# Fewer multiplications in a graph network: two basis products in 15 block products, the second root product and the output product in 7

## The chip, the cores and the metric

The kernel runs on one core of one Trainium2 chip. The metric is the device time of one execution in microseconds (us). Three runs of the kernel before took 716.10, 716.02 and 715.76 us; their median is 716.02 us. One further execution was taken with the profiler, and every duration quoted here is from that one.

## The reference

A graph with 384 nodes and 12,672 edges goes through an attention layer (1024 features, 16 heads) and then through a relational network of two layers with 768 features. Only the second part matters here. All numbers are fp32.

```python
x = relu(h_text @ w_in + b_in)                   # [384, 1024] @ [1024, 768]
for l in range(2):
    h_in = x
    W = einsum('rb,bio->rio', comp[l], basis[l])  # 6 relations from 4 bases
    # messages per relation and edge, each divided by the count of its (relation, target),
    # summed by target; then:
    x = agg + h_in @ root[l] + conv_bias[l]
    x = relu(x) + h_in
    x = batchnorm(x)                             # over the 384 nodes
h_final = x @ w_out + b_out                      # [384, 768] @ [768, 1024]
out = x_after_attention + layernorm(h_final)
```

The kernel does not build the six relation matrices. It multiplies x with each of the four bases (four products of 384 x 768 with 768 x 768 per layer, called H), and it mixes the six count-normalised adjacency matrices A into four matrices At, one per basis, by the coefficients comp. The aggregate is then the sum over bases and nodes of At and H.

## The kernel before, in words

**Engines.** The matrix engine (PE) takes a stationary operand of 128 x 128 and a moving operand of 128 x N, and adds into one of eight PSUM banks. A `matmul` in the code shows as two records of PE in the profile. The vector engine (DVE) and the scalar engine (ACT) read PSUM and write SBUF. The order on PE, DVE, ACT, POOL and SP is the order of the Python code (`manual_schedule`), so an instruction that waits holds back all that stand behind it on its engine. A helper `next_bank` gives out the bank that has been out of use the longest.

**Block products.** Most products are already made by a scheme of Winograd: a product of 2 x 2 blocks takes seven block products in place of eight, and four sums on each side before them. Blocks are halves of the features, or of the nodes.

**Input product (L848 to L903).** It makes XT, x transposed, in three passes p of two feature tiles. In a pass the scalar engine copies a first block product out of PSUM, DVE adds a second one (`add_up_quad`, L882), and the scalar engine applies relu (L883); all further copies of the pass stand behind that relu on the scalar engine. After pass 0, DVE makes the four sums for pass 2 (`output_sums`, L396).

**The four bases of a layer (loop over b, L971 to L1010).** The 384 nodes are three tiles of 128. Two of them form the 2 x 2 scheme; the third is multiplied plainly. `node_sums` (L920) makes the four sums of x once per layer; `weight_sums` (L927, L929) and `last_sums` (L935) make the four sums of each basis. A basis is 33 matmuls with N = 384: 18 at L985 and 15 at L979. A basis comes from memory in three parts of 768 KB (`wload`, L85), into a pool of five buffers; SP issues a load when the buffer's last reader is done. Between the block products of layer 0, `share` (L361 to L367) turns counts into means, and `mix` (L346, L348) makes At. The counts are scattered by POOL until 386.3 us; then POOL issues twelve loads of them into the tile A.

**Root product and aggregate.** `pr[o]` receives root times x in 36 matmuls with N = 384 (L1019), and then a part of the aggregate in the same banks; `begin` copies it out. The aggregate's sums of At (L1082 to L1086) and of H (`feature_sums`, L1097), its products (`times`, L1077), the additions into XN (`take`, L1107), relu (`rectify`, L1110), the residual and the statistics (`measure`, L1042 to L1049) and the batch norm (`normalise_layer`, L1054 to L1058) follow in three passes p of two feature tiles.

**Output product (L1169 to L1198).** For each node tile t: 12 matmuls with N = 512 (tile 2: 6 with 512 and 12 with 256), then on DVE the addition of b_out, the statistics (L1187, L1189), and the layer norm with the residual (L1194 to L1197), then the store. `x_sb` holds the residual; POOL adds the layer norm's beta to it (L1170).

Of the kernel before, what the change touches and what calls it, by code (L numbers as in the profile page):

```python
# [10 lines left out]
F32 = mybir.dt.float32  # L11
# [6 lines left out]
P = 128  # L18
N = 384
# [9 lines left out]
HC = DC // 2  # L29
HN = N // 2  # L30
# [14 lines left out]

BQ, BK, BV, BIQ, BIK, BIV, B_IN, CB, GAM, BET, NCOL = 0, 8, 16, 24, 32, 40, 48, 54, 66, 78, 90
# [5 lines left out]
def gnn_kernel(ctx: ExitStack, tc: tile.TileContext, out, x, edges, chunks, cols, rows, small,  # L52
               wq, wk, wv, wiq, wik, wiv, wo, w_in, basis, root, w_out):
# [299 lines left out]
    def add_up(r):  # L353
        sums[r] = late.tile([P, N], F32, tag="sum", name="sum", bufs=4)
        nc.gpsimd.tensor_tensor(sums[r], A[:, r, 0, :], A[:, r, 1, :], ALU.add)
        nc.gpsimd.tensor_tensor(sums[r], sums[r], A[:, r, 2, :], ALU.add)

    def share(r):
# [3 lines left out]
        rn = late.tile([P, N], F32, tag="rn", name="rn", bufs=2)  # L362
# [9 lines left out]
    with ExitStack() as inner:  # L372
# [263 lines left out]
        A = late.tile([P, R, NT, N], F32, tag="A", name="A")  # L636

# [93 lines left out]
        for g in range(STEPS + 1):  # L731
# [14 lines left out]
            if f + 2 == STEPS:  # L746
# [4 lines left out]
                w_first = [wload(basis[0, 0, part], (2, DC), "w_c") for part in range(3)]  # L751
                w_first += [wload(basis[0, 1, part], (2, DC), "w_c") for part in range(2)]
# [117 lines left out]
        node_sum(T, 4, h2T, T4)  # L870
        rest = lambda: None
        for p in range(3):
# [23 lines left out]
            if p == 0:  # L896
                output_sums(a[2], S[0])

# [7 lines left out]
    with tc.tile_pool(name="conv", bufs=1) as cp:  # L906
# [7 lines left out]

        def node_sums(X):
            S = cp.tile([P, 4, 3, P], F32, tag="S", name="S")
            for i, a, b, op in ((0, block(X, 1, 0), block(X, 1, 1), ALU.add), (1, S[:, 0], block(X, 0, 0), ALU.subtract),
                                (2, block(X, 0, 0), block(X, 1, 0), ALU.subtract),
                                (3, block(X, 0, 1), S[:, 1], ALU.subtract)):
                nc.vector.tensor_tensor(S[:, i], a, b, op)  # L920
            return S

        def weight_sums(w):
            T13 = keep.tile([P, 3, 2, HC], F32, tag="hT", name="T13")
            T2 = keep.tile([P, 3, HC], F32, tag="mask8", name="T2")
            for c in range(3):
# [5 lines left out]
        def last_sums(w, T2):  # L932
            T4 = cp.tile([P, 3, HC], F32, tag="T4", name="T4")
# [4 lines left out]
        w_first = [w_first[:3], w_first[3:]]  # L938

        def load_basis(l, b):  # L940
            w = w_first.pop(0) if w_first else []
            return w + [wload(basis[l, b, part], (2, DC), "w_c") for part in range(len(w), 3)]
# [15 lines left out]

        def go_between(*site):
            between.pop(site, lambda: None)()  # L960

        S = node_sums(XT)
        w = load_basis(0, 0)
        T = weight_sums(w)
        for l in range(L):
# [3 lines left out]
            for b in range(B):  # L969
# [23 lines left out]
                times(pc, S[:, 0], lambda c: T[0][:, c], True)  # L993
# [3 lines left out]
                times(pa, S[:, 1], lambda c: T[1][:, c])  # L997
                nc.scalar.copy(hs[0][1], pa)
                times(pc, S[:, 3], lambda c: w[c][:, 1, HC:])
                nc.vector.tensor_tensor(hs[0][1], hs[0][1], pc, ALU.add)  # L1000
                times(pa, S[:, 2], lambda c: T[2][:, c])
# [12 lines left out]
            w = [wload(root[l, part], (2, DC), "w_c") for part in range(3)]  # L1014
            XN = xtp.tile([P, KC, N], F32, tag="XT", name="XN")
            pr = [next_bank("ps_c", [i for i in range(8) if i not in kept])[:, :N] for _ in range(KC)]
            for k in range(KC):
# [6 lines left out]
            room2 = keep.tile([P, KD * N], F32, tag="hT", name="room2")  # L1024
            spaces = [room2[:, 2304:]]
            if l + 1 < L:
                spaces += [v.rearrange("p i k o -> p (i k o)")[:, i * 768:(i + 1) * 768] for v, n in
                           ((cp.tile([P, 4, 3, P], F32, tag="S", name="sums"), 2),
                            (wpool.tile([P, 2, 6, P], F32, tag="w", name="sums"), 2)) for i in range(n)]
# [240 lines left out]
```

## Time and profile before

| | |
|---|---|
| median of three runs | 716.02 us |
| the profiled execution | 717.47 us |
| its span, first to last instruction | 715.7 us |
| PE busy | 699.9 us (98%) |
| DVE busy | 512.6 us (72%) |
| ACT busy | 157.6 us (22%) |
| POOL busy | 308.1 us (43%) |
| mean granted PE clock | 0.995 |

The span is what the page's shares refer to. The profiled execution's own time is 1.8 us longer than its span, and the median of the plain runs lies 0.3 us above the span.

How to read it: a stage has a stretch of time, and in it each engine has a busy time. Busy time of PE close to the length of the stretch means that PE was the limit there. "Idle before, releaser" tells how long an engine stood still ahead of an instruction, and what let it go on. A line ending in L402 or L85 is that of a helper used by many stages, so the tile's name tells the stage: ps_x is the input product, ps_g the bases, ps_c root and aggregate, ps_f the output.

### The profile page before, as it was taken

What the parts mean: (1) busy time and instruction counts of PE and PEld (TensorE: products, weight loads), DVE (VectorE), ACT (ScalarE), POOL (GpSimd) and SP (SyncE); (2) the same over time, 40 slices, a digit from 0 to 9 for tenths busy, and PEclk for the clock granted to TensorE, in tenths of its full rate; (3) what the DMA queues carried; (4) which work ended last, traced back from release to release, by engine and by line L of the source; (5) the groups of instructions that cost most, each with busy time, mean ns of one, the idle gap of its engine ahead of it and who ended that gap; (6) DMA issues with size and microseconds to landing.
All of it is one profiled execution on the core that took longest, in us unless ns stands there. A gap on an engine that the chain in (4) does not pass through costs nothing.

```text
span 715.7 us, 9149 instructions
## 1 busy us (share of the span) xinstructions
PE 699.9 (98%) x3228; PEld 527.9 (74%) x3228; DVE 512.6 (72%) x1307; ACT 157.6 (22%) x360; POOL 308.1 (43%) x239
## 2 busy tenths in 40 slices
PE   8999999999999999999999999999999999999995
PEld 7759999999997444478985555558975555579943
DVE  5886697868886699787534279798878766507756
ACT  3211111111111577410221124202131111011100
POOL 1366777778687788687786542000000000120000
PEclk9999999999999999999999999999999999999999
DMA  8788787373562622733424994311104322700001
GB/s 303 267 279 264 228 250 212 80 243 67 203 209 43 177 2 1 221 44 45 89 0 103 250 288 153 133 44 45 45 0 133 102 69 94 308 1 1 1 30 59
DMA packets 69180, 91.04 MB, mean 127 GB/s; under 512 B 22940, under 2 KB 50688, under 8 KB 68750
## 3 DMA queue, kind: packets, MB, share of 16 engines
q1 hardware_dynamic: 46830, 78.45, 32.6%
q0 software_dynamic: 21296, 9.60, 10.8%
q10 hardware_dynamic: 1008, 2.41, 0.9%
q8 instruction: 25, 0.41, 0.2%
q14 instruction: 21, 0.17, 0.1%
HBM read 79.27 MB, written 11.16 MB: 126 GB/s over the span
## 4 chain that ended last, share of the span: by engine, by line
PE 87%; DVE 10%; ACT 2%; DMA 1%; issue 0%; DVEq 0%; ACTq 0%
PE ps_g L985 12%; PE ps_g L979 10%; PE ps_k L402 10%; PE ps_c L1077 10%; PE ps_v L402 8%; PE ps_q L420 6%; PE ps_q L402 5%; PE ps_f L1183 4%; DVE At L348 4%; PE ps_y L402 3%; PE ps_c L1019 3%; PE ps_x L402 3%; PE ps_o L707 2%; PE ps_s L662 2%; PE ps_pT L696 2%; PE ps_v L586 2%
## 5 line engine op out<-in xcount | busy, mean ns | idle before, releaser
L283 POOL DMA_INDIRECT atab<-count,at x99 | 166.3, 1679 | 44.2 <-issue 23.5
L278 POOL DMA_INDIRECT mtab<-m_val,at x99 | 103.4, 1045 | 57.6 <-issue 22.9
L1170 POOL TENSOR_TENSOR x_sb<-x_sb,room 128x1024 f32<-128x1024 f32 x3 | 7.0, 2348 | 188.9 <-DMA room<-in_rows 188.9
L348 DVE SCALAR_TENSOR_TENSOR At<-A,small_sb,At 128x1152 f32<-128x1152 f32 x40 | 53.6, 1414 | 0.0
L979 PE MATMUL ps_g<-T,S 128*128 128x384 f32 x144 | 49.1, 486 | 0.0
L985 PE MATMUL ps_g<-w_c,XN 128*128 128x384 f32 x144 | 47.7, 487 | 1.1 <-DVE XN L1107 1.1
L985 PE MATMUL ps_g<-w_c,XT 128*128 128x384 f32 x144 | 47.9, 486 | 0.0
L420 PE MATMUL ps_q<-hT,w_q 128*128 128x384 f32 (+1 forms) x160 | 43.4, 435 | 1.4 <-DVE hT L108 1.4
L985 PEld LDWEIGHTS ps_g<-w_c,XN 128*128 128x128 f32 x144 | 27.3, 190 | 20.2 <-DVE XN L1107 1.4
L979 PEld LDWEIGHTS ps_g<-T,S 128*128 128x128 f32 x144 | 27.3, 190 | 19.2 <-ACT H L991 0.4
L985 PEld LDWEIGHTS ps_g<-w_c,XT 128*128 128x128 f32 x144 | 27.3, 190 | 18.8
L420 PEld LDWEIGHTS ps_q<-hT,w_q 128*128 128x128 f32 x160 | 30.1, 200 | 14.1 <-ACT hT L101 1.7
L1077 PE MATMUL ps_c<-At,H 128*128 128x192 f32 x216 | 36.4, 326 | 0.0
L1077 PEld LDWEIGHTS ps_c<-At,H 128*128 128x128 f32 x216 | 35.4, 190 | 0.5
L402 PE MATMUL ps_k<-T,S 128*128 128x192 f32 x192 | 35.1, 326 | 0.0
L1107 DVE TENSOR_TENSOR XN<-XN,ps_c 128x192 f32<-128x192 f32 x38 | 12.5, 349 | 30.8 <-ACT XN L1063 19.7
L402 PEld LDWEIGHTS ps_k<-T,S 128*128 128x128 f32 x192 | 31.8, 190 | 0.0
L1183 PE MATMUL ps_f<-w_out,XN 128*128 128x512 f32 (+1 forms) x84 | 31.1, 531 | 0.0
L675 DVE CUSTOM_DVE_ANT_0 s<-ps_s,mask 128x384 f32<-128x384 f32 x48 | 24.5, 550 | 5.3 <-PE ps_s L662 5.3
L267 DVE SCALAR_TENSOR_TENSOR same<-cells,own,later 128x128 f32<-128x128 int32 x99 | 28.0, 350 | 0.4
L267 DVE SCALAR_TENSOR_TENSOR same<-keys,key,weigh 128x128 f32<-128x128 int32 x99 | 27.9, 349 | 0.0
L1183 PEld LDWEIGHTS ps_f<-w_out,XN 128*128 128x128 f32 x84 | 15.9, 190 | 14.9 <-issue 14.3
(298 smaller groups left out, 1411.6 us busy)
## 6 DMA issues: line engine op xcount, KB each, us to landing
w_c<-in_basis SPq DMA_DIRECT2D x96, 192.0 KB, 4.1
atab<-zero SPq DMA_DIRECT2D x36, 192.0 KB, 5.2
A<-atab POOLq DMA_DIRECT2D x12, 576.0 KB, 9.0
keys<-keys_d SPq DMA_DIRECT2D x25, 192.0 KB, 5.1
w_c<-in_root SPq DMA_DIRECT2D x6, 768.0 KB, 7.1
w_q<-in_wiq SPq DMA_DIRECT2D x16, 256.0 KB, 6.4
w_k<-in_wk SPq DMA_DIRECT2D x16, 256.0 KB, 5.8
w_k<-in_wik SPq DMA_DIRECT2D x16, 256.0 KB, 3.0
```

Source lines behind the costliest of these rows:

```text
L267: nc.vector.scalar_tensor_tensor(same, row[:, n, :], mine[:, c:c + 1], times, ALU.is_equal, ALU.mult, accum_out=count[:, i, c:c + 1])
L278: nc.gpsimd.indirect_dma_start(mtab[c // PER][:, :], bass.IndirectOffsetOnAxis(at[:, 0, c:c + 1], 0), m_val[:, c:c + 1], None)
L283: nc.gpsimd.indirect_dma_start(atab[0 if i < 11 else i % 2][:, :], bass.IndirectOffsetOnAxis(at[:, 1, c:c + 1], 0), count[:, 1, c:c + 1], ...
L348: nc.vector.scalar_tensor_tensor(At[:, b], A[:, r], w, At[:, b], ALU.mult, ALU.add)
L402: nc.tensor.matmul(ps, a[:, k, :], b[:, k, :], start=start and k == 0, stop=(k == 3), skip_group_check=not start)
L420: nc.tensor.matmul(ps[o][:, c], wt_[:, k, o * P:(o + 1) * P], src[:, k, c], start=(k == 0 and c.start == 0), stop=(k == KD - 1 and c.stop ...
L675: nc.vector.tensor_tensor_reduce(s[j], ps[:, :N], mask8[:, t, :], -scale, 3.0e38, ALU.add, ALU.min, tops[:, j:j + 1])
L979: nc.tensor.matmul(ps, x[:, c], y(c), start=start and c == 0, stop=(c == 2), skip_group_check=not start)
L985: nc.tensor.matmul(ps, block(XT, n, i)[:, c], w[c][:, i, o * HC:(o + 1) * HC], start=(first and c == 0), stop=(c == 2 and (i == 1 or ps is ...
L1019: nc.tensor.matmul(pr[o], w[k // 2][:, k % 2, o * P:(o + 1) * P], XT[:, k, :], start=(k == 0), stop=(k == KC - 1))
L1077: nc.tensor.matmul(ps, x[:, c], y[:, c], start=start and c == 0, stop=stop and c == 5, skip_group_check=True)
L1183: nc.tensor.matmul(p, XT[:, k, t * P:(t + 1) * P], w[k // 2][:, k % 2, c0:c1], start=(k == 0), stop=(k == KC - 1))
```

## The change

1. **Bases 0 and 1 of layer 0** are made by a scheme for blocks of 3 x 2 and 2 x 3: three node tiles, two halves of the input features, three thirds of the output features. A plain product has 18 block products; the tables PRODUCTS, X_SUMS and W_SUMS give one with 15. Each block product is three matmuls with N = 256, added to one of four running sums c, each in a bank of its own; after a block product, the running sum is copied into, added to or taken from one or two of the nine output blocks of H. 11 sums of x are made once, 10 sums of weights per basis. DVE makes two sums of each kind in pass 1 of the input product, and the rest between the block products, by a table of steps. (A row of PRODUCTS names the block of x, the block of weights, the running sum, and the blocks of H with their signs.) In the second basis, DVE also makes `node_sums` and the first nine sums of basis 2, whose loads move ahead as well.
2. **The root product of layer 1** is made by the 2 x 2 scheme in three passes: 63 matmuls with N = 192. DVE's sums of At for the aggregate move between its passes; the sums of x and the first sums of root move into basis 3, and the part of the aggregate that was added in the root's banks gets three banks of its own.
3. **The output product** is made by the 2 x 2 scheme for node tiles 0 and 1: 21 matmuls with N = 512 in place of 24. Tile 2 stays plain. Its sums of weights are made by DVE during the aggregate of layer 1, its sums of x ahead of the product.
4. Layer norm's beta is added to x_sb by DVE in the three passes of the input product (128 x 1024 each); the row is loaded into boB before. POOL's three additions at L1170 go.
5. Tiles that were allocated anew (T13, T2, S, T4, sums) become fixed places: room2, mroom, x_all, w_room, sum_room.

```diff
+X_SUMS = (
+    (6, 1, 2, -1, 4),
+    (7, -1, 5, -1, 6),
...
+W_SUMS = (
+    (6, 1, 2, 1, 5, -2),
+    (7, 1, 1, 1, 6, -1),
...
+PRODUCTS = (
+    (2, 1, 0, ((4, 1),)),
+    (6, 6, 1, ((7, 1), (8, -1))),
+    (7, 7, 0, ((7, 1),)),
+    (5, 8, 2, ((7, 1),)),
+    (9, 9, 1, ((6, -1),)),
+    (10, 10, 0, ((8, -1),)),
+    (3, 4, 3, ((4, 1),)),
+    (11, 5, 0, ((5, -1),)),
+    (12, 12, 3, ((3, -1),)),
...
+    (0, 15, 3, ((1, -1),)),
+    (16, 3, 0, ((6, -1),)),
+)
...
-                w_first = [wload(basis[0, 0, part], (2, DC), "w_c") for part in range(3)]
-                w_first += [wload(basis[0, 1, part], (2, DC), "w_c") for part in range(2)]
+                for b, t in ((0, 2), (0, 1), (0, 0), (1, 2), (1, 1)):
+                    load_third(b, t)
+                nc.sync.dma_start(boB, rows[R_LNB:R_LNB + 1, :].to_broadcast([P, D]))
...
             if p == 0:
                 output_sums(a[2], S[0])
+            elif p == 1:
+                for i, x in enumerate(X_SUMS):
+                    if x[0] in (6, 14):
+                        sum_features(i)
+                for i in range(2):
+                    sum_weights(0, i)
+                    free_from[0, i] = 99
+            nc.vector.tensor_tensor(x_sb[:, p, :], x_sb[:, p, :], boB, ALU.add)
...
+        def bases_by_15():
+            todo = [(g * NPROD + w[5], 1, g, i) for g in range(BY_15) for i, w in enumerate(W_SUMS) if g or i > 1]
...
+            todo += [(first[x[0]] - 3, 2, 0, i) for i, x in enumerate(X_SUMS) if x[0] not in (6, 14)]
+            todo = sorted(todo + [(NPROD + k, 3, 0, 0) for k in (4,)] + [(NPROD + k, 4, 0, c) for c, k in enumerate((7, 8, 13))])
+            for step in range(NPROD * BY_15):
...
+                while todo and todo[0][0] <= step:
...
+                x, w, c, targets = PRODUCTS[k]
...
+                for j in range(3):
+                    nc.tensor.matmul(ps, x[:, j], w[:, j], start=start and j == 0, stop=(j == 2),
+                                     skip_group_check=not start)
+                for to, sign in targets:
...
+                    if (g, to) in begun:
+                        nc.vector.tensor_tensor(dst, dst, ps, ALU.add if sign > 0 else ALU.subtract)
+                    elif sign > 0:
+                        nc.scalar.copy(dst, ps)
...
+                if (g, k) == (0, 7):
+                    load_third(1, 0)
+                elif (g, k) in ((0, 10), (0, 14), (1, 8)):
+                    basis_loads.append(wload(basis[0, len(basis_loads)], (2, DC), "w_c"))
...
+        def second_root(rest):
+            root_w.append(wload(root_thirds[2], (KC, HC2), "w_c"))
...
+            for p in range(3):
...
+                times(pa, root_block(p, 0, 0), x_quarter(0, 0), True)
+                nc.scalar.activation(quads[0][0], pa, AF.Identity, bias=bs[0])
+                rest()
+                times(pb, root_block(p, 0, 1), x_quarter(1, 0), True)
+                nc.vector.tensor_tensor(quads[0][0], quads[0][0], pb, ALU.add)
+                times(pc, s[:, 0], T[0], True)
+                nc.scalar.activation(quads[1][1], pc, AF.Identity, bias=bs[1])
+                if p < 2:
+                    root_S.append(root_sums(p + 1))
+                times(pa, s[:, 1], T[1])
+                nc.scalar.activation(quads[0][1], pa, AF.Identity, bias=bs[0])
+                times(pc, s[:, 3], x_quarter(1, 1))
+                nc.vector.tensor_tensor(quads[0][1], quads[0][1], pc, ALU.add)
+                if p:
+                    next(shares_)
+                times(pa, s[:, 2], T[2])
+                nc.vector.tensor_tensor(quads[1][1], quads[1][1], pa, ALU.add)
+                if p:
+                    next(shares_)
...
+                out_sums((0, 0), (1, 0), (0, 1), (1, 1))
...
+                if l + 1 == L:
+                    out_sums(*(((0, 2), (1, 2), (2, 2), (3, 2)) if last else ((2, p),)))
                 times(pc, S[p][3], q(1, 1))
...
+                if l + 1 == L:
+                    out_sums((3, p))
...
-        for t in range(NT):
-            nc.gpsimd.tensor_tensor(x_sb[:, t, :], x_sb[:, t, :], rowsB[:, 2, :], ALU.add)
...
+        third(*parts[0], *range(KC - 1))
+        pa, pb, pc, pd = [next_bank("ps_f") for _ in range(4)]
+        times(pa, block(XT, 0, 0), b_end(0, 0), True)
+        put_out(0, 0, pa, True, False)
+        times(pb, block(XT, 0, 1), b_end(1, 0), True)
+        put_out(0, 0, pb, False, True)
+        times(pc, OS[0], summed(0), True)
+        put_out(1, 512, pc, True, False)
+        times(pa, OS[1], summed(1))
+        put_out(0, 512, pa, True, False)
+        times(pc, OS[3], b_end(1, 1))
+        put_out(0, 512, pc, False, True)
+        times(pd, block(XT, 1, 1), summed(3), True)
+        put_out(1, 0, pd, True, False)
+        times(pa, OS[2], summed(2))
+        finish(0)
+        put_out(1, 0, pa, False, True)
+        put_out(1, 512, pa, False, True)
+        third(*parts[0], KC - 1)
+        for p, c0 in parts[1:]:
+            third(p, c0, *range(KC))
+        finish(1)
+        for p, c0 in parts:
+            put_out(2, c0, p, True, True)
+        finish(2)
```

`put_out` is one DVE addition out of PSUM, with two statistics of 256 columns where its last argument says so. `finish(t)` is the layer norm and the store of node tile t, the same instructions as L1194 to L1198.

## The prediction

> **What bounds the kernel now.** I read the page first: the span, the busy times and the chain by engine.
>
> ```profile
> span 715.7 us, 9149 instructions
> PE 699.9 (98%) x3228; PEld 527.9 (74%) x3228; DVE 512.6 (72%) x1307; ACT 157.6 (22%) x360; POOL 308.1 (43%) x239
> PE 87%; DVE 10%; ACT 2%; DMA 1%; issue 0%; DVEq 0%; ACTq 0%
> ```
>
> PE is busy 98% of the span, so work taken from PE is worth its time unless another engine then comes last. DVE at 72% is the candidate. Then the busy times by stage (columns: PE, PEld, DVE, ACT, POOL, with instructions, then PE clock, DMA share, GB/s): input product, bases 0, 1 and 2, aggregate of layer 1, output product, tail.
>
> ```profile
> 341.11:370.89 29.78, 29.14 (x177) 28.02 (x177) 12.21 (x25) 7.97 (x22) 23.43 (x16) 1.00 0.34 49
> 370.89:392.18 21.29, 21.29 (x67) 12.55 (x67) 10.73 (x18) 2.81 (x6) 14.88 (x10) 1.00 0.38 63
> 392.18:413.45 21.27, 21.27 (x67) 12.53 (x67) 7.43 (x13) 2.87 (x6) 12.13 (x12) 1.00 0.97 254
> 413.45:434.76 21.31, 21.31 (x68) 12.47 (x67) 16.87 (x16) 6.05 (x12) 10.45 (x11) 1.00 1.03 270
> 636.34:677.29 40.95, 40.95 (x253) 40.95 (x253) 24.36 (x69) 6.78 (x16) 0.00 (x0) 1.00 0.00 1
> 677.29:708.20 30.91, 30.91 (x84) 15.61 (x83) 18.13 (x44) 1.13 (x4) 0.00 (x0) 1.00 0.09 34
> 708.20:715.70 7.50, 0.02 (x1) 0.00 (x0) 4.08 (x9) 0.20 (x1) 0.00 (x0) 0.78 0.19 71
> ```
>
> In these stages PE never rests, and DVE has 10 to 14 us to spare in each. The DMA share near 1 in bases 1 and 2 is POOL's loading of A. The chain in order of time (start, length) gives PE's pace and one place where DVE already decides:
>
> ```profile
> 355.88 0.28 DVE XT L882
> 356.18 0.36 ACT XT L883
> 356.54 0.32 ACT XT L888
> 356.90 11.98 PE ps_x L402 x72
> ...
> 370.89 11.61 PE ps_g L985 x36
> 677.29 30.94 PE ps_f L1183 x84
> ```
>
> The timeline of DVE shows one wait for weights in base 2, and the last addition of the output product:
>
> ```profile
> 418.74 0.96 DVE L927 TENSOR_TENSOR T<-w_c 128x768 f32<-128x768 f32 x1 [3.70 <-DMA w_c<-in_basis]
> 708.26 0.42 DVE L1187 TENSOR_TENSOR hf<-ps_f,room 128x256 f32<-128x256 f32 x1 [1.70 <-PE ps_f L1183]
> ```
>
> [...] 11.61/36 is 322.5; for N = 192, 162.5 (68.90 us for 424 records in the chain: 162.5). [...] N = 256 is 216 ns (16 records of L840 took 3.45 us) and N = 512 is 429. [...] 768 columns take 952 ns and 384 take 558, a slope of 1.03 ns. [...] w_c loads landed after 2.2 to 14.2 us, the late ones beside A's.
>
> **What PE saves.** Bases 0 and 1: 66 records of 322.5 are 21.29 us each; 45 matmuls, 90 records of 216.5, are 19.49. Two bases: -3.6. Root: 72 x 322.5 = 23.22; 126 x 162.5 = 20.48: -2.7. Output: 30.94; the scheme has 42 records of N = 512 and tile 2 has 12, so 54 x 429 + 24 x 216.5 = 28.37: -2.6. In all -8.9 us.
>
> **What comes back.** For each touched stretch I laid out the instructions in the changed order: each starts when its engine is free and its inputs are there. Durations are the rows' own (DVE 768 columns .95, 384 .56, 512 .69, 1152 1.36, PSUM addition .35 at 192 columns and .42 at 256; ACT .41), DVE instructions overlap by .07 where independent, a handover takes .05, and a PSUM result follows the next start by .16. Laid out so, the old input product ends at 370.80 (370.72 measured), and the old stretch from the second root to the last DVE instruction has the output product start 66.1 us in (65.9) and the tail end 35.41 us later (677.12 to 712.54 is 35.42).
>
> *Input product, +1.2.* Beta's addition (1.22 us, the row of L540) stands on DVE between the sums and pass 1's first addition, which starts right behind the sums (the 355.88 above). Behind it wait relu, the copy at L888, and PE at 356.90. Nothing hides 1.22 less .07 overlap. In passes 1 and 2 the additions and four early sums (4.1 us) end before PE needs what follows. POOL's removed additions hid behind PE: 0. The row's DMA comes after 20 loads that SP ends at 343.1; landing 6.2 us later, it is there before 356; the cover is 6 us.
>
> *Bases 0 and 1, +2.0.* DVE's work per pair: 18 weight sums (17.1), 9 sums of x (5.0), node_sums (2.2), basis 2's sums (4.5), 20 additions (8.4): 37 us in 39. A product reads a running sum's bank only after the last copy from it. So PE waits where DVE is behind: at product 8 of base 0 for the addition of product 6 (.3), and at product 7 of base 1, because between products 3 and 5 DVE has node_sums and two weight sums, 4.1 us, ahead of product 5's addition, and PE offers 3.9 less what was late already: 1.05. Last, base 2's first matmul takes the bank that base 1 used first; its wait on DVE stands in the changed order. That bank's last addition follows the last product: .16 + .05 + .42 + .05 = .7, where before the next basis followed at once.
>
> *The late weights, +0.6.* Ahead of that addition DVE has the third part of basis 2's sums. Its load can go out only when product 7 of base 1 has freed a buffer, at about 403.3 on the old clock. Loads beside A's took 7.2 us here (411.5, when basis 1's buffer came free, to 418.7) and 8.6 (387.04 to 395.68). So the part lands at 410.5 to 411.9; DVE gets there at 410.6. Waiting 0 to 1.3, I take .6. Before, this wait held DVE alone; now it holds PE. Then DVE enters base 2 with the sums done, 4.5 us and the old 3.70 us wait ahead; shares and mix have more room, but the mix starts after base 3 in any case and is as long as before: 0.
>
> *Second root and aggregate, +1.5.* Basis 3 gets 5.2 us more DVE on 12.8 in 21.4: covered. In the root, the last addition of pass 1 stands behind a sum of At (1.36): .2, and .1 at the start. In the aggregate, DVE goes from 24.4 to about 33 us in 41, by 12 sums of w_out (.69 each). Where such a sum stands ahead of a `take`, PE waits for the bank: in pass 1 .2 and .4, in pass 2 .5. Three new takes and the early sums of At hide.
>
> *Output and tail, +3.7.* PE ends 28.4 us after the product's start, not 31.0, but DVE is the later one. Tile 1's last blocks and tile 2 come out together: pd ends at 19.75 us, and from 19.96 DVE has in this order: one addition (.62), finish(0) 3.33, two blocks with statistics 1.44 each, finish(1) 3.33, tile 2's three parts 1.44 + .81 + .88, and finish(2) 3.32: 16.6 in all, with no wait for PE. It ends at 36.55, where the old tail ended at 35.41. So the stretch is 1.1 longer, and PE's 2.6 is lost too.
>
> **Sum.** -8.9 + 1.2 + 2.0 + 0.6 + 1.5 + 3.7 = +0.1 on a span of 715.7. The median of the plain runs stands 0.3 above that span; +0.1 on 716.02 is 716.1 us. Changes below 0.2% (1.4 us) are about what this measurement cannot tell from none.
>
> **Rivals.**
>
> *PE's saving mostly arrives.* My waits in bases and aggregate hang on .2 to 1 us of DVE lateness; if DVE catches up there, 2.0 + .6 + 1.5 fall away, and 716.1 becomes 712.0. For it: before, DVE waited for PE 31.2 us at L1000. Against it: the layout met the old times within .2. If also the tail were no longer than PE's, 708.3; its DVE list is too plain for that.
>
> *The late part of basis 2.* This one ends slower. Loads beside A's took up to 14.2 us. Landing at 416 in place of 411.2 puts 4.8 us on PE's path at the start of base 2: 720.9. It decides from a landing at 412.6 on, which brings 717.5. For it: DMA share .97 to 1.03 there. Against it: the three loads ahead of it go out before 392, so less is queued.
>
> *DVE does not keep up in the bases.* 37 of 39 us leaves little; dependent sums cost .1 more each. Ten such would make 717.1.
>
> That the change removes nothing can be excluded: the order has the 45 matmuls per basis.
>
> **How the numbers follow.** The forecast, gains eaten: .50 (714.5 to 717.6 its own range); saving mostly arrives, 710 to 714.5: .24; late part or slow bases, 717.5 to 722: .22; full saving .02; worse .02. The range 712.3 to 719.6 leaves out about a fifth. Faster by over 0.2% (below 714.6): .27; slower (above 717.4): .25; between: .48.
>
> **What would show it.** In the chain: DVE XT ahead of PE in pass 1 about 1.2 us later; waits of PE ps_g on DVE H of about 1 us at product 7 of base 1 and .7 or more at base 2, with DVE T idle for w_c just before; base 2 starting between 413.0 and 414.3. The last PE matmul some 8 us ahead of DVE's last instruction, not 4.5; DVE without gaps there. The prediction is wrong if PE waits for neither, or if the last part lands after 412.6.

## The result, and the profile after

The changed kernel took 720.7 us (median of 13 runs, 716.4 to 724.25), the kernel before beside it 716.05 us (13 runs, 715.76 to 717.84). The ratio is 1.0056, with a 95% interval of 1.0039 to 1.0072: slower by over 0.2%, and outside the range given. Here and below, a ratio and its interval compare only those runs of each kernel that lie within 1.5% of its own fastest run. The profiled execution took 722.45 us.

The page of the changed kernel gives the span, the busy times and the chain by engine:

```profile
span 720.7 us, 9459 instructions
PE 693.3 (96%) x3324; PEld 541.5 (75%) x3324; DVE 557.5 (77%) x1385; ACT 160.2 (22%) x372; POOL 302.4 (42%) x236
PE 80%; DVE 14%; ACT 2%; issue 1%; DMA 1%; SPq 0%; DVEq 0%; ACTq 0%
```

PE is busy 6.6 us less (8.9 were forecast; slower matmuls, shown below, take back 2.6) and DVE 44.9 us more, and DVE's share of the chain went from 10% to 14%. Who held PE between 330 and 470 us stands in the waits (total, times, longest, in us):

```profile
PE ps_g L1244 <- DVE H L1100: 5.5, 1, 5.5
PE ps_x L452 <- ACT XT L980: 1.2, 1, 1.2
PE ps_g L1094 <- DVE H L1100: 0.7, 1, 0.7
```

The 1.2 us in the input product and the 0.7 us inside the bases were forecast. The 5.5 us stand before base 2's first matmul, where 1.3 were forecast (0.7, and 0.6 for the late weights). DVE's timeline there (start, length, line, output and inputs, idle time before it):

```profile
408.02 0.75 DVE L1100 TENSOR_TENSOR H<-H,ps_g 128x256 f32<-128x256 f32 x2 [0.54 <-PE ps_g L1094]
412.65 1.77 DVE L1033 TENSOR_TENSOR room<-w_c 128x768 f32<-128x768 f32 x1 [3.88 <-issue]
414.45 1.23 DVE L1035 TENSOR_TENSOR mroom<-w_c,room 128x384 f32<-128x384 f32 x1
415.61 0.41 DVE L1100 TENSOR_TENSOR H<-H,ps_g 128x256 f32<-128x256 f32 x1
```

L1033 and L1035 are the two sums of the third part of basis 2, L1100 below them is the addition that frees the bank. DVE first stands idle for 3.88 us, with no releaser that the profile could name, and then takes 3.0 us for sums that take 0.95 and 0.56 elsewhere. At the same time POOL's timeline has a sum of A (L405), which took 1.58 us in place of 0.99:

```profile
412.89 1.30 POOL L911 DMA_DIRECT2D A<-atab  x1
413.69 1.58 POOL L405 TENSOR_TENSOR sum_room<-A 128x384 f32<-128x384 f32 x1
415.34 1.20 POOL L406 TENSOR_TENSOR sum_room<-sum_room,A 128x384 f32<-128x384 f32 x1
```

What follows the pause is dear too. Busy times by stretch (PE, PEld, DVE, ACT, POOL, then PE clock, DMA share, GB/s):

```profile
400.00:408.00 8.00, 8.00 (x37) 7.07 (x38) 6.86 (x11) 1.51 (x4) 5.49 (x5) 1.00 1.03 196
408.00:416.00 8.00, 2.57 (x12) 1.91 (x11) 4.07 (x6) 0.38 (x1) 3.83 (x4) 0.90 1.06 371
416.00:424.00 8.00, 7.93 (x17) 4.49 (x18) 1.90 (x4) 0.56 (x1) 5.10 (x6) 0.67 1.14 265
```

Between 416 and 424 PE is busy and makes 17 records, at a mean granted clock of 0.67: up to 421.3 its records of 384 columns start 0.640 us apart, and 0.3225 after that.

By stages, from the first matmul of one to the first of the next (from the two traces):

| stage, us | before | after | change | forecast |
|---|---|---|---|---|
| input product | 29.78 | 30.91 | +1.13 | +1.2 |
| four bases of layer 0 | 87.99 | 93.84 | +5.85 | -1.0 |
| rest of layer 0 | 69.00 | 69.00 | 0 | 0 |
| bases of layer 1 | 83.31 | 83.31 | 0 | 0 |
| second root and aggregate | 66.11 | 64.58 | -1.53 | -1.2 |
| output product to the end | 38.57 | 39.64 | +1.07 | +1.1 |
| from the input product on | 374.75 | 381.27 | +6.52 | +0.1 |

The input product itself began 1.5 us earlier (339.40, not 340.94), which makes +5.0 of the span. The bases of layer 0 hold all of the miss.

### The profile page after: what moved, and what is told of

It reads as the page before. It is cut to its first block, busy times and chain, and to the rows that moved or that the text cites. A ratio compares the mean times of both kernels' runs of the same rounds, so it can differ in the third digit from the quotient of the medians.

```text
span 720.7 us, 9459 instructions
## 1 busy us (share of the span) xinstructions
PE 693.3 (96%) x3324; PEld 541.5 (75%) x3324; DVE 557.5 (77%) x1385; ACT 160.2 (22%) x372; POOL 302.4 (42%) x236
## 4 chain that ended last, share of the span: by engine, by line
PE 80%; DVE 14%; ACT 2%; issue 1%; DMA 1%; SPq 0%; DVEq 0%; ACTq 0%
PE ps_k L452 10%; PE ps_g L1244 10%; PE ps_v L452 8%; PE ps_g L1238 8%; PE ps_c L1347 7%; PE ps_q L470 6%; PE ps_q L452 5%; DVE At L398 4%; PE ps_g L1094 4%; PE ps_y L452 3%; PE ps_x L452 3%; PE ps_c L1182 3%; PE ps_o L758 2%; PE ps_f L1479 2%; PE ps_s L713 2%; PE ps_pT L747 2%
## 5 line engine op out<-in xcount | busy, mean ns | idle before, releaser
L470 PE MATMUL ps_q<-hT,w_q 128*128 128x384 f32 (+1 forms) x160 | 41.8, 422 | 1.4 <-DVE hT L158 1.4
L470 PEld LDWEIGHTS ps_q<-hT,w_q 128*128 128x128 f32 x160 | 28.5, 190 | 14.1 <-ACT hT L151 1.7
L1244 PE MATMUL ps_g<-w_c,XT 128*128 128x384 f32 x72 | 26.9, 527 | 5.5 <-DVE H L1100 5.5
L1244 PEld LDWEIGHTS ps_g<-w_c,XT 128*128 128x128 f32 x72 | 14.8, 208 | 16.5 <-DVE H L1100 5.9
L1238 PE MATMUL ps_g<-room,x_all 128*128 128x384 f32 x72 | 25.2, 486 | 0.0
L1281 PE MATMUL ps_c<-XT,w_c 128*128 128x384 f32 x72 | 23.5, 486 | 0.0
L758 PE MATMUL ps_o<-At,v 128*64 128x384 f32 x96 | 20.8, 512 | 1.3 <-ACT attT L761 1.3
L713 PE MATMUL ps_s<-k,q 64*128 64x384 f32 x96 | 21.5, 528 | 0.0
L416 DVE RECIPROCAL sum_room<-sum_room 128x384 f32<-128x384 f32 x6 | 15.3, 2549 | 7.5 <-ACT sum_room L415 7.5
L1033 DVE TENSOR_TENSOR room<-w_c 128x768 f32<-128x768 f32 x18 | 17.9, 996 | 3.9 <-issue 3.9
```

Source lines behind the costliest of these rows:

```text
L470: nc.tensor.matmul(ps[o][:, c], wt_[:, k, o * P:(o + 1) * P], src[:, k, c], start=(k == 0 and c.start == 0), stop=(k == KD - 1 and c.stop ...
L713: nc.tensor.matmul(score[g][j][:, :N], q2[ho, hc, t * P:(t + 1) * P], k2[ho, hc, :], start=True, stop=True)
L758: nc.tensor.matmul(pso[p][j * HD:(j + 1) * HD, :N], v2[:, m, h * HD:(h + 1) * HD], turned(g)[:, j, :], start=(m == 0), stop=(m == NT - 1))
L1238: nc.tensor.matmul(ps, x[:, c], y(c), start=start and c == 0, stop=(c == 2), skip_group_check=not start)
L1244: nc.tensor.matmul(ps, block(XT, n, i)[:, c], w[c][:, i, o * HC:(o + 1) * HC], start=(first and c == 0), stop=(c == 2 and (i == 1 or ps is ...
```

## The experiments

In most of the runs below the stages ahead of the input product were longer, and the kernel before took longer beside them too (medians of 728 to 750 us in place of 716, which is called its usual pace below); their times scattered by 10 us and more. So I compare the stages from the input product's first matmul, each from one profile: those that nothing touched were 69.0 and 83.3 us in every profile. The code cuts are shortened. "Base 0 to 2" is the stretch from base 0's first matmul to base 2's.

### Is it the load?

`e8_A_later`: the block that loads A goes behind the bases in the code, and POOL waits for base 1.

```
+ if (g, k) == (1, 13): nc.gpsimd.tensor_copy(scrap, H_[:, 1, targets[0][0] // 3, :1])
- (ahead of the input product) all nc.gpsimd.dma_start(A[...]) and add_up
+ (behind bases_by_15) the same
```

> The changed kernel with POOL's loads of A held back until product 13 of base 1 (POOL copies one column of H first, and the loads stand behind it), about 17 us later than before. Nothing but the third part's load is then under way from 401.5 to 408.5. Theory 'the late part': the load lands in 4 to 5 us, before DVE gets there at 408.8, DVE's idle time ahead of that sum is 0 to 0.3 us, and PE waits at most 2.5 us before base 2 (the part's two sums, 1.5 us, and the addition still stand there). Rival (DVE's 3.9 us are not the load, as the profile names no releaser for them): the idle time stays at 3 us or more. The whole time tells nothing here: the shares of A come 17 us later and PE will wait for them in base 2 or 3.

DVE's timeline:

```profile
429.53 0.95 DVE L1025 TENSOR_TENSOR room<-w_c 128x768 f32<-128x768 f32 x1
430.52 0.56 DVE L1027 TENSOR_TENSOR mroom<-w_c,room 128x384 f32<-128x384 f32 x1
```

No idle time, usual lengths, and PE waited 0.5 us. Base 0 to 2 took 40.8 us. The load's last piece landed at 427.09 in the trace, 4.7 us after its first was issued and 2.4 us before DVE came. (PE later waited 7.7 us for the shares of A, as had to be expected.) That takes away A's transfers and A's sums together; the next run parts them.

`e13_only_A_sums`: the loads of A stay, and only POOL's sums of them wait for base 1.

```
- for r in range(R): accumulate A[r]; load the next; if 0 < r < 5: add_up(r - 1)
+ for r in range(4): accumulate A[r]; load the next
+ if (g, k) == (1, 12): nc.gpsimd.tensor_copy(scrap, H_[:, 1, targets[0][0] // 3, :1])
+ (behind the bases) for r in range(4): add_up(r); if r > 1: accumulate A[r + 2]
```

> The changed kernel with POOL's sums of A held back until product 12 of base 1, and nothing else: the third part's sums stay ahead of the last addition. It parts the two causes. If the load's landing matters by itself, DVE stands idle ahead of that sum and PE's wait before base 2 is above 2.0 us; if the landing is in time, the two sums (1.5 us) start at about 0.6 us ahead of the last product's end and PE waits 1.4 to 1.6 us, the stretch from base 0 to base 2 taking 41.6 to 41.9. Theory 'both': up to the last product the stretch is 40.2 to 40.4, as clean as in the kernel with both repairs, and what is above comes from the wait for the load alone. Rival (POOL's sums don't matter without the other repair): 42 or more up to the last product.

```profile
414.31 0.96 DVE L1031 TENSOR_TENSOR room<-w_c 128x768 f32<-128x768 f32 x1 [3.66 <-issue]
415.30 0.56 DVE L1033 TENSOR_TENSOR mroom<-w_c,room 128x384 f32<-128x384 f32 x1
```

The sums have their usual length again, but DVE idles as long as before, and PE waits 3.8 us. Up to the last product the stretch is 40.3 us, as "both" said; bases 2 and 3 took 47.1 us, 1.6 above 45.5, at a clock of 0.79 behind the pause. Timed: 1.0061 (1.0031 to 1.0091). So the idle time is the load, even though the profile calls it "issue". The trace's landings agree: the part comes in four pieces, the last of which landed at 412.57 in the changed kernel and at 414.23 here, 0.08 us ahead of DVE's start each time.

`e9_as_changed`: the changed kernel once more.

> The changed kernel once more, as it is, for a second trace of bases 0 and 1. Theory 'the late part' with 'POOL and DVE slow each other' (a DVE sum of two tensors in SBUF is made late by a sum of A that POOL is making, and the reverse): PE waits 2 to 6 us before base 2, its length differs from the first trace's 5.5 us with what of A's transfers and sums falls beside it, and each DVE sum that takes more than 1.2 times its usual time overlaps a sum of POOL's (lines L405 and L406). Rival (DVE slows beside transfers): slow DVE sums stand where POOL makes no sum.

PE waited only 1.0 us before base 2, but 2.2 and 0.9 us inside base 1; base 0 to 2 took 43.9 us, where the first trace had 45.8. The late sums and POOL's:

```profile
443.64 2.36 DVE L1035 TENSOR_TENSOR mroom<-w_c,room 128x384 f32<-128x384 f32 x1
445.92 1.75 DVE L1033 TENSOR_TENSOR room<-w_c 128x768 f32<-128x768 f32 x1
```

```profile
444.04 1.54 POOL L405 TENSOR_TENSOR sum_room<-A 128x384 f32<-128x384 f32 x1
445.65 1.20 POOL L406 TENSOR_TENSOR sum_room<-sum_room,A 128x384 f32<-128x384 f32 x1
```

Every slow DVE sum of the stretch overlaps a sum of POOL's. So PE is held up by two causes, in shares that change from run to run.

### Is it the place in DVE's queue, and the bank?

`e1_sums_last` moves the third part's sums behind the last addition:

```
- [(NPROD + k, 4, 0, c) for c, k in enumerate((7, 8, 13))]
+ [(NPROD + k, 4, 0, c) for c, k in enumerate((7, 8))]
+ (behind the loop over products) third.append(weight_sums(basis_loads, 2))
```

> The changed kernel with one step moved: the third part of basis 2's sums (T13(2) and T2(2)) is made after the last addition of base 1, not before it. Theory 'the late part' (DVE stands at that sum until the part's load has landed, and the addition that frees base 2's first bank stands behind it): PE's wait before base 2 falls from 5.5 us to about 0.7, the clock granted after it is 1.00 again in place of 0.67, so some 4.8 + 2.8 us leave the profiled execution (722.45): 714 to 715.5, and the runs, which spread from 716.4 to 724.25, come within about 2 us of each other. Rival 'DVE is late as a whole' (its work for bases 0 and 1 has piled up, and the sum is only where it shows): the addition is still late, PE waits 3 us or more, 718 or more. Rival 'the time is lost elsewhere' (tail, aggregate): the wait goes and the median stays above 718.

`e2_other_bank` leaves DVE's order and turns the five banks of base 2 by one, so that `pa` gets a free one:

```
+ if (l, b) == (0, BY_15): five = five[1:] + five[:1]; taken[:] = taken[1:] + taken[:1]
```

> The changed kernel with another bank for base 2's first matmuls: pa gets one that base 0 had freed, and the bank that base 1's last product adds up in goes to pc, which starts some 11 us later. DVE's order stays. Theory 'the late part': PE no longer waits at base 2's start (0 to 0.1 us), while DVE still stands idle for 2 to 5 us ahead of the third part's sum; the time is 713.5 to 715.5, as with the sums moved or 0.7 less. Rival (PE needs what DVE makes there, or the weights themselves are late for PE): PE waits 3 us or more at another matmul of base 2, and the time stays above 718.

With the sums last, PE waited 0.52 us before base 2; with the other bank 0 us, although DVE still idled 1.1 us ahead of the sum. In both, bases 2 and 3 took 45.5 and 45.4 us (48.08 in the changed kernel). So in these traces a late load costs PE nothing unless that addition stands behind it and PE needs just that bank. The idle 1.1 us are fewer than the 2 to 5 expected: the load was less late against DVE here. The times said nothing there (750.45 and 752.21 us beside 750.34). Base 0 to 2 was 43.5 and 42.9 us, not the clean 40.8, and that led to POOL's sums.

`e1b_sums_last` and `e1c_sums_last` are the first of them timed again:

> The kernel with the third part's sums behind base 1's last addition, timed again where the kernel before runs at its usual pace. Theory 'the late part': PE's wait before base 2 is 0.5 to 0.7 us, as it was in the first look, the clock stays at 1.00, and the median is 714 to 715.5 where the kernel before has 716.05 (ratio 0.997 to 0.9995, against 1.0056 for the change as it is), with the runs within 2 us. Rival 'the time is lost elsewhere': the wait is gone, but the ratio stays above 1.002.

> The changed kernel with only the third part's sums moved behind base 1's last addition, timed where the kernel before runs at its usual 716 to 717. Theory 'the late part': PE's wait before base 2 is 0.5 to 0.7 us, the clock stays, and 5 to 7.5 us of the changed kernel's profile leave: 714.5 to 717 as a median, a ratio of 0.998 to 1.002 against 1.0056. Base 0 to base 2 takes 41 to 44 us, by how many of POOL's sums of A fall beside DVE's, so the runs may still lie 3 us apart. Rival (the wait for A's sums, which held PE 3.6 us when they were made later, is there anyway): PE waits 2 us or more at the first share, and the ratio stays above 1.003.

The wait was 0.5 us both times, and bases 2 and 3 took 45.5 us. The ratios were 0.9998 (0.9919 to 1.0078) and 0.9995 (0.9965 to 1.0024), the second against a kernel before at 727.57 us, so neither at the usual pace. The first lies just outside the theory's range and the second inside, with intervals wider than the question, so the times decide nothing and the traces alone carry this.

### What does a long pause of PE cost?

`e6_pause_long`: the sums last, and ahead of the last addition `weight_sums` of part 0 four times more.

```
+ [(NPROD + 13, 5, 0, 0)] * 4        # weight_sums(basis_loads, 0) again
```

> The kernel with the third part's sums moved behind the last addition, and the sums of the first part (1.5 us a time) made four times more ahead of that addition; the values stay the same. It puts back a pause of PE at base 2's start that no load has a part in: DVE has 6.1 us to do from 408.8, so PE waits 4.5 to 5 us. Theory 'a long pause costs twice' (after it PE is granted a lower clock for some us): 4 us for the pause and 2 to 3 us for the clock, 6 to 7 us above the kernel without it, and the window after the pause shows a clock well below 1. Rival (the low clock came from the transfers beside it): 4 us, clock 1.00.

PE waited 7.4 us, more than planned, since two of the repeated sums met sums of POOL. Busy times by stretch:

```profile
432.00:440.00 8.00, 0.83 (x4) 0.38 (x2) 7.79 (x8) 0.00 (x0) 5.90 (x6) 0.89 1.07 344
440.00:448.00 8.00, 7.79 (x17) 4.47 (x18) 2.99 (x6) 0.58 (x1) 3.90 (x5) 0.69 1.06 261
```

The clock is 0.69 after the pause, and bases 2 and 3 took 47.89 us, 2.4 above the 45.5 of `e1_sums_last`, the kernel without it; from the input product on the difference is 6.5 us. No load made this pause, but A's transfers still ran beside it (DMA share 1.06), so this run alone does not exclude them. Two others do. In `e1c_sums_last`, the same kernel as `e1_sums_last`, they ran there as well (DMA share 1.11 from 424 to 432 us, around base 2's start), without a long pause, and the clock was 1.00. And in `e4_beta_pool`, below, PE paused for 4.5 us with no transfers at all (DMA share 0.00), and the clock was 0.59 behind the pause:

```profile
682.70:690.00 7.30, 7.24 (x27) 7.24 (x28) 4.00 (x10) 0.00 (x0) 0.00 (x0) 0.59 0.00 1
```

So in these runs the low clock comes behind the long pause, with transfers and without. Behind it the records start about twice their usual distance apart: 0.640 for 0.3225 us at 384 columns in the changed kernel; twelve records of 192 columns took 4.21 us for 2.11 in `e4_beta_pool`, and six of 256 columns 2.93 us for 1.46 in `e11_beta_in_gaps`. In the changed kernel they stay so from 416.07 to 421.3, 5.2 us; in the other runs, by what the pauses cost there and at half the pace, it is some 3 to 6 us, an estimate. Pauses up to 2.2 us (`e9_as_changed`) left what follows at its length: in `e2_other_bank`, with waits of 2.1 and 1.2 us, base 0 to 2 took 42.9 us, 3.3 more than the clean 40.8 less its own waits of 0.7 and 0.5. Those of 3.3 (`e11_beta_in_gaps`), 3.8 (`e13_only_A_sums`), 4.5 (`e4_beta_pool`), 5.5 (the changed kernel) and 7.4 us (here) cost about 2.9, 1.6, 3.0, 2.6 and 2.4 us more.

### What do POOL's sums of A cost?

`e10_A_sums_later` has both repairs, the sums last and POOL's sums later:

> The third part's sums behind the last addition, and POOL's sums of A (two of 1 us for each of the first four tables) held back until product 12 of base 1 is through; the loads of A stay where they were, except that two of the last come later. Theory 'POOL and DVE slow each other': no DVE sum in bases 0 and 1 takes more than 1.1 times its usual time, and the stretch from base 0's first matmul to base 2's is 40.3 to 41.2 us, where the kernel with the sums moved alone showed 43.5 and 42.7, and the kernel with A's loads held back altogether 40.8. Rival (A's transfers slow DVE, not POOL's sums): 42.5 to 43.5 as before. PE may wait up to 1 us for the first share of A in base 2.

Base 0 to 2 took 40.8 us, and no DVE sum in it was slow; bases 2 and 3 took 45.5. From the input product on it is 373.8 us, 1.0 less than before the change (timed, 744.65 us beside 747.55, with a scatter of 17 us). What the two engines contend for was not shown, but it is not every DVE instruction that POOL's sums slow: in `e9_as_changed` five additions out of PSUM that DVE made beside POOL's sum at 450.18 took 1.74 us in all, their usual time, while the two sums of tensors in SBUF shown there were stretched 1.8 and 4.2 times (1.75 us for 0.95, 2.36 for 0.56).

`e4_beta_pool` shows it at its worst. It was meant to test another step, the +1.2 of the input product: beta added by POOL after the last layer, as before the change.

```
- nc.vector.tensor_tensor(x_sb[:, p, :], x_sb[:, p, :], boB, ALU.add)     # input product
+ for t in range(NT): nc.gpsimd.tensor_tensor(x_sb[:, t, :], x_sb[:, t, :], rowsB[:, 2, :], ALU.add)
```

> The sums moved, and beta added to x_sb by POOL after the last layer, as before the change, instead of by DVE in the input product. Theory 'beta's addition costs what the prediction says': the wait of PE for XT at pass 1 goes from 1.2 us to 0.1 or less, and the time is 1.1 to 1.3 us below the kernel with the sums moved. Rival (DVE's work there hides, or the time comes back in base 0, where DVE gives what comes next): less than 0.4 us. POOL is idle from the second layer on, so its three additions should cost nothing.

The input product fell from 30.91 to 29.78 us, so the step's size is right. But root and aggregate rose from 64.6 to 72.2 us. The timeline, POOL's three additions and DVE's sums of features (0.95 us each when alone):

```profile
672.55 9.08 POOL L1446 TENSOR_TENSOR x_sb<-x_sb,room 128x1024 f32<-128x1024 f32 x3 [207.76 <-DMA room<-in_rows]
673.41 3.00 DVE L1362 TENSOR_TENSOR room<-room,H 128x768 f32<-128x768 f32 x1
676.33 3.10 DVE L1362 TENSOR_TENSOR H<-H 128x768 f32<-128x768 f32 x1
679.36 3.09 DVE L1362 TENSOR_TENSOR room<-H,room 128x768 f32<-128x768 f32 x1
```

While sums and additions stand beside each other, DVE's three sums take 9.2 us in place of 2.9, and POOL's three additions 9.08 in place of the 6.96 of the kernel before. PE waited 4.5 us for the `take` behind them, and its next 24 records took 7.25 us in place of 4.2. The ratio was 1.0198 (1.0132 to 1.0265). "POOL is idle there, so it should cost nothing" was wrong.

`e11_beta_in_gaps` keeps beta on DVE, but right behind a pass's first addition:

```
- nc.vector.tensor_tensor(x_sb[:, p, :], x_sb[:, p, :], boB, ALU.add)     # end of a pass
+ for t in ((), (0,), (1, 2))[p]: nc.vector.tensor_tensor(x_sb[:, t, :], x_sb[:, t, :], boB, ALU.add)
```

> The third part's sums behind the last addition, and DVE adds beta to x_sb right behind a pass's first addition in the input product (tile 0 in pass 1, tiles 1 and 2 in pass 2), where it stood idle 2.4 and 3.3 us, not at the end of each pass. Theory (beta's 1.2 us cost what stands behind them, not DVE's time as such): PE's wait for XT at pass 1 falls from 1.2 us to 0.1 or less, the input product from 30.9 to 29.8 us, and nothing comes back later. Rival (the additions of pass 1 or 2 are then late): 30.5 us or more.

The input product took 29.79 us, as before the change: there beta costs nothing. But base 0 to 2 took 46.3 us in this profile: DVE met POOL's sums in node_sums and in the sums of the second basis, PE waited 3.3 us in base 1, and the clock was 0.82 after it. (The ratio, 1.0065 with 1.0028 to 1.0102, counts 12 of 20 runs beside 5 of 43; the medians of all are 746.9 and 747.55 us.)

### Is the tail DVE's?

`e3_old_output`: the sums last, and the output product as before the change, with no sums of w_out in the aggregate.

```
- out_sums(...) at all five places; OS, put_out, finish and the seven block products
+ the loop over node tiles of the kernel before
```

> The sums moved as in the kernel beside it, and the output product made as before the change: 78 matmuls' worth of whole blocks, no sums of w_out in the aggregate, no sums of the features at its head. Theory 'the tail is DVE's' (the output product in seven saves PE 2.6 us that nobody waits for, the tail is 0.7 to 1.1 us longer, and the sums of w_out cost 1.1 us in the aggregate): 1.5 to 2.2 us faster than the kernel beside it, 712 to 714. Rival 'the output product's saving arrives': 1 to 2.6 us slower than the kernel beside it, 715.5 to 718.

The aggregate took 63.73 us in place of 64.58, and from the output product's first matmul to the end 38.76 in place of 39.64: 1.7 us less, though PE had 31.09 us to do there and not 28.52. So the output product in seven is a loss of 1.7 us. (The times, 1.0075 with 0.9998 to 1.0151, don't resolve this.)

`e7_all_three` is `e4_beta_pool` with `finish(0)` ahead of tile 1's first block:

```
+ finish(0)
  put_out(1, 0, pd, True, False)
  times(pa, OS[2], summed(2))
- finish(0)
```

> Beta on POOL and the sums moved, and in the output product DVE finishes tile 0 (its normalisation and store, 3.33 us) before it takes tile 1's first block, not after. Theory 'the tail is DVE's': DVE stands idle 1.1 us ahead of that block now; that idle time is filled, everything behind it comes 1.0 to 1.1 us earlier, and PE's two later products still have their banks: 1.0 us less than with beta on POOL alone. With all three the median is 711.5 to 713.5 where the kernel before has 716.05. Rival (PE then waits for pd or pa, and the tail is PE's): no gain or up to 1 us slower than with beta on POOL alone.

The last DVE instruction came 35.57 us after the output product's start, 36.43 in `e4_beta_pool`: 0.9 of the 1.0 expected. The rest of the kernel carries POOL's 7 us, and the ratio is 1.0061 (0.9967 to 1.0155).

### A version that beats both?

`e12_best` has both repairs, beta in the gaps and the old output product:

> The sums of the third part last, POOL's sums of A later, beta in the gaps, and the output product as before the change. By the stages of the profiles so far: input product 29.8, bases 0 and 1 to base 2's start 40.8, bases 2 and 3 45.5, rest of layer 0 69.0, bases of layer 1 83.3, root and aggregate 63.7, output to the end 38.8: 370.9 us from the input product's first matmul, where the kernel before has 374.75 and the changed kernel 381.3 in its first profile. So about 3.8 us, 0.5%, faster than the kernel before: a ratio of 0.993 to 0.997. If POOL's sums then hold PE up in base 2, 372 to 373.

It took 370.89 us from the input product on, as worked out (before: 374.75); timed, 0.9993 (0.9814 to 1.0173). Where the kernel before ran at 717.45 us, it and `e10_A_sums_later` went again:

> The best kernel so far, timed again: 370.9 us from the input product's first matmul as before, and a median 3 to 4.5 us below that of the kernel before beside it.

> The whole change with both repairs (the third part's sums last, POOL's sums of A later), timed again: 373.8 us from the input product's first matmul, a median 0.5 to 2.5 us below that of the kernel before.

Both fell through: 1.0070 (1.0023 to 1.0117) and 1.0057 (1.0005 to 1.0110). The waits of PE, of `e12b_best` and of `e10b_sums_later`:

```profile
PE ps_cnt L411 <- POOL sum_room L406: 9.4, 1, 9.4
```

```profile
PE ps_cnt L411 <- POOL sum_room L406: 3.6, 1, 3.6
```

Base 0 to 2 was clean (40.8 us both), but with A's transfers later against PE there, POOL's sums held back were too late for the first share, and PE was slow behind the pause again: in `e12b_best`, after the 9.4 us, its next 14 records took 6.40 us, and the 14 after them, of the same shapes, 4.52. Where the stages ahead were longer, A was ready earlier against PE, and this had not shown. So the last two leave POOL's sums where the change has them: `e14_bases_and_root` is the sums last, beta in the gaps and the old output product, and `e15_shares_later` calls each share one place later as well.

```
- between = {(0, 2, 0): shares(0), (0, 2, 1): shares(1), (0, 2, 2): shares(2), (0, 2, 4): share(3), mix(0, 0), ...
+ between = {(0, 2, 1): shares(0), (0, 2, 2): shares(1), (0, 2, 4): shares(2), (0, 3, 0): share(3), mix(0, 0), ...
```

> The third part's sums last, beta in DVE's gaps, the output product as before the change; POOL's sums of A where the change has them. Against the kernel with the sums moved alone: 1.1 us less in the input product, 0.85 in the aggregate, 0.9 in the output, together 2.8: 712 to 714.5, a ratio of 0.994 to 0.998. Rival: bases 0 and 1 give the input product's gain back, since DVE and POOL meet more there: 714.5 or more.

> As the kernel beside it, with each share of A called one place later in bases 2 and 3, so that sums of A that come late don't hold PE at its first share. If they hold it there, this kernel is 1 to 4 us faster than the one beside it; if they don't, the two are within 0.5 us, or this one is up to 1 us slower because the mix behind base 3 waits for the last share.

Both took 370.9 us from the input product on, 3.9 less than the kernel before, with these waits of PE in `e14_bases_and_root`:

```profile
PE ps_g L1094 <- DVE H L1100: 0.7, 1, 0.7
PE ps_g L1245 <- DVE H L1100: 0.5, 1, 0.5
```

These 370.9 us are not yet the kernel's. Up to base 2 `e14_bases_and_root` has the code of `e11_beta_in_gaps`, whose profile took 46.3 us from base 0 to 2 where these two took 40.8. What differs is when POOL's sums begin: 21.1 us after base 0's first matmul in `e11_beta_in_gaps`, 30.5 and 34.4 us here. By these traces, where they fall decides whether PE waits, and that changes from run to run.

Timed beside a kernel before at 727.57 us, the ratios are 1.0002 (0.9973 to 1.0031), outside the 0.994 to 0.998 expected, and 0.9917 (0.9880 to 0.9953). The second looks like a gain, but it counts only 11 of that kernel's 22 runs, since one took 714.76 us, and 43 of 51 of the kernel before. The medians of all runs are 727.27 and 726.17 us, the second 0.2% below the kernel before. PE waited for no share of A in either profile. So no version is shown to beat the kernel before.

## Why the prediction was wrong

**The failed step is "The late weights, +0.6".** It named the place, the instruction and the order behind it, and DVE came to the sum at 408.8, as laid out (410.6 on the prediction's clock, which has base 0 at 372.1, where the trace has it at 370.5). One size was misread and two were missing:

- The load. Issued at 401.5, as laid out, it landed its last piece at 412.57, 11.0 us later; the step took 7.2 to 8.6. Of PE's 5.5 us this is 3.5: 5.5 less 0.5 that stay and 1.5 that come next. `e13_only_A_sums`, with the load alone, gives 3.8 less 0.5.
- POOL. The two sums took 3.0 us, not 1.5, beside a sum of A. Every duration in the layout was that of a row standing alone. Before the change DVE was busy for 18.2 of the 42.6 us of these bases and could hide this; the 37 us of work in 39 that the prediction counted left next to nothing.
- The clock. A pause was priced at its own length, in the rival too (4.8 us of lateness at 4.8); behind the 5.5 us bases 2 and 3 took 2.6 us more than in the runs without a long pause.

The 7.2 us come from a misreading. They were counted from 411.5, but the load that L927 waited for until 418.74 had gone out in four pieces from 408.33 on. In the trace before the change, the issues on SP, and who waited for them:

```profile
408.33 2.36 SPq L85 DMA_DIRECT2D w_c<-in_basis  x4
  DVE T L927: 3.7, 1
```

That is 10.4 us, and 403.3 + 10.4 is 413.7 on the prediction's clock, 3.1 us behind DVE where 0.6 was taken. So the trace that the prediction was made from already held most of the late load.

3.5 + 1.5 + 2.6 = 7.6 us, of which 0.6 was forecast. The rest came out. Input product +1.13 for +1.2. Bases 0 and 1 without the last wait took 40.26 us; the forecast was 39.0 of PE's work, .3 and 1.05 of waits, 40.3. From start to start of its records PE lost 0.28 us at product 8 of base 0 and 0.96 at product 7 of base 1, so the places are right too. PE's records of 256 and 512 columns start 0.216 and 0.429 us apart in the trace of the changed kernel (twelve each from 406.53 to 409.12 and from 685.32 to 690.47), as priced. Root and aggregate -1.53 for -1.2, with 0.37 us lost in the root (.3 forecast) and 0.18, 0.24 and 0.43 in the aggregate (.2, .4 and .5); output and tail +1.07 for +1.1, with PE's last matmul 7.7 us ahead of DVE's last instruction (8 forecast). `e10_A_sums_later`, with the failed step taken away, is 1.0 us below the kernel before, where the forecast less its 0.6 says 0.5.

**The rivals.** "The late part of basis 2" was the right one, and that its time of 720.9 is near the median is luck. Its price was not right: for the landing that came, 414.2 on its clock, it gives 719.1, since it added the lateness alone. "DVE does not keep up in the bases" is in it as well: its cause was given as .1 us for dependent sums, and was POOL. "PE's saving mostly arrives" fell: the waits that it did without came, in the bases, the root and the aggregate.

**What stays open.** Why the input product began 1.5 us earlier was not tried. The spread of the plain runs (716.4 to 724.25) fits the two profiles' 43.9 and 45.8 us from base 0 to 2, the second with a lowered clock behind it. The mean clock on record for each run goes with it: 0.992 to 0.995 in the five runs under 719 us, 0.987 to 0.991 in the six over 721. But only profiles show stages, so this is argued. Whether `e14_bases_and_root` or `e15_shares_later` is faster than the kernel before at its usual pace was not measured.

## What to carry to other kernels

When DVE is given work up to the length of its stage, look at what POOL does there, and price DVE's sums of tensors in SBUF at their length beside POOL's, not alone: 1.8 to 4.2 times as long in `e9_as_changed` and `e4_beta_pool`. Put a sum that waits for a load behind every instruction that the busiest engine needs. And price a pause of PE of 3.3 us or more at 1.6 to 3 us more than its length, as it was here; up to 2.2 us it cost its length alone. Time a load from the issue of its first piece to the landing of its last.

## What was not expected of the hardware

- Sums in SBUF on DVE and on POOL stretch each other: a DVE sum of 768 columns went from 0.95 to 3.0 to 3.1 us beside POOL's additions of 1024 columns, and POOL's three from 6.96 us (in the kernel before) to 9.08.
- The profile can show a wait for a load in several pieces as "issue" (3.88 and 3.66 us, in the changed kernel and `e13_only_A_sums`), though the last piece landed 0.08 us ahead of DVE's start; in the kernel before, the same kind of wait (3.70 us) was put down to the DMA.
- After pauses of 3.3 (`e11_beta_in_gaps`), 4.5 (`e4_beta_pool`) and 5.5 us (the changed kernel) PE's next records took about twice their usual time, in the changed kernel for 5.2 us; after pauses of 3.3 to 7.4 us the profile's mean clock over the next 7 to 13 us was 0.59 to 0.82.
